# A decoder kernel turns its cross-attention contexts on VectorE and through DRAM instead of on TensorE

## The chip, the cores and the metric

The kernel runs on one core of a Trainium2 chip. The metric is the device time of one execution in microseconds; the time shown is the median of three runs. The profile is that of one further execution. Engines are named as in the profile: PE is TensorE (PEld its weight loads), DVE is VectorE, ACT is ScalarE, POOL is GpSimd, and SP is the engine whose queue issues all DMAs of this kernel.

## The reference

The reference is two decoder layers over `x` of shape (32, 56, 128), all in fp32. Both layers attend to the same context `ctx_1024` of shape (32, 1500, 128), and a layer normalization follows every block.

```
x = LN(x + windowed_self_attention(x))            # 16 heads of 8, window 32
x = LN(x + cross_attention_0(ctx, ctx, x))        # one head of 128, softmax over 1500 keys
x = LN(x + experts_0(x))                          # 8 experts of 512, top 2, gelu
x = LN(x + recurrent_mixer(x))                    # convolution, gates, a scan over 56 steps
x = LN(x + cross_attention_1(x, ctx))             # 16 heads of 64, softmax over 1500 keys
x = LN(x + experts_1(x))                          # shared expert and 8 of 256, top 2, silu
```

A context is the 1500 x 128 block of one of the 32 batches. Scores need it with the 128 features on the partitions ("turned"), and the weighted sum over keys needs it with the keys on the partitions, as it lies in DRAM.

## The kernel before

**Contexts.** A context is loaded as 125 partitions of 12 keys (`PK = 125`, `CK = 12`), key number 12p + c on partition p in chunk c, by `load_context` (two DMAs). `cxN` holds the two contexts of a pair for the first cross attention, `amN` those for the second one, each with a column of ones beside the 128 features, so that one product gives the weighted sum and the normalizer.

**Stages.** Two batches make a pair; there are 16 pairs. The groups are pair 0, pair 1, and then seven groups of two pairs (`GROUPS`). For each group a thread `pre` runs self attention, `cross_attention_0`, `experts_0`, the recurrent mixer and the queries of the second cross attention. The thread `attention` (called main) does the second cross attention for 32 batches in 64 blocks of 512 or 384 query columns: for each of 12 chunks a product of `amT` (the turned context, 125 columns of it as the stationary operand) and the queries gives scores `s`; maxima, exponentials and the products `v` with `amN` follow one block later. The thread `post` does the output projection and `experts_1`. The first two groups run in an opening of their own (`opening`), pair 1 in borrowed tiles ("aside", where `amN` takes the place of `cxN`).

**Order.** The threads are Python generators. A clock, `clock["pe"]`, adds up an assumed cost of each matmul; every `yield` of a thread gives a delay on this clock before which the thread is not resumed (`HOP`, `NORM`, `LOAD`), and `until` resumes `pre` as far as its share of `PRE_US` is due by the progress of main. Within what this writes down, the tile framework orders the instructions of each engine. [...]

**Turning.** `cross_attention_0` turns the two contexts of a pair with 12 transposes each (`tr`, L156 in the profile: the context is the stationary operand, an identity the moving one), four to a PSUM bank. Three copies per context, two on ACT and one on DVE (L518), bring them to `cxT`, which are the tiles `big0` and `big1`. A DMA stores each turned context to the DRAM tile `memT` (L520), from where `load_attended_T` fetches it into `amT` when the second cross attention comes to that batch (L1062). `amT` has one buffer. The score products of `cross_attention_0` (qpad, 500 columns each) read `cxT`; its probabilities `pr` overwrite `cxT[0]` and are turned back by 12 transposes into `pt`, which lies in `cxT[1]`. Then the 24 products with `cxN` follow, and the contexts of the next pair are loaded into `cxN`. The code of the score loop of main (`mm` is L147 in the profile):

```
ps = bank(p_s, "s")
mm(ps[:PK, :n], amT[:, c * PK : (c + 1) * PK], qT)
nc.scalar.copy(s[:, c, :], ps[:PK, :n])
```

Of the kernel before, what the change touches and what calls it, by code (L numbers as in the profile page):

```python
# [9 lines left out]
F32 = mybir.dt.float32  # L10
# [4 lines left out]
B, S, D, SK = 32, 56, 128, 1500  # L15
# [6 lines left out]
GROUPS = [[0], [1]] + [[p, p + 1] for p in range(2, NPAIR, 2)]  # L22
# [6 lines left out]
PK, CK = 125, 12  # L29
PSPLIT = 112  # L30
NS, CS = 3, 4
# [29 lines left out]
CYCLE = 1 / 2400  # L61
MATMUL_MIN, TRANSPOSE = 0.23, 0.145

PRE_US, POST_US, PAIR_US = 74.0, 31.0, 80.5
PROJECT_US = 3.6
BLOCKS = ((0, 512), (512, 384))

# [2 lines left out]
def decoder_kernel(  # L70
# [19 lines left out]
    nc = tc.nc  # L90
# [15 lines left out]
    def bank(pool, tag):  # L106
        if pool is p_f and place["aside"]:
            pool, tag = p_s, "s"
        return pool.tile([P, 512], F32, tag=tag, name=tag)
# [44 lines left out]
    def tr(ps, in_):  # L154
        k = in_.shape[0]
        nc.tensor.transpose(ps, in_, ident[:k, :k])  # L156
        clock["pe"] += TRANSPOSE
# [19 lines left out]
    n1 = const.tile([P, H1, D], F32, name="n1")  # L177


    cxN = [const.tile([PK, CK, D + 1], F32, name=f"cxN{i}") for i in range(2)]  # L180
    amN = [const.tile([PK, CK, D + 1], F32, name=f"amN{i}") for i in range(2)]
    amT = const.tile([P, CK * PK], F32, name="amT")
    for t in (*cxN, *amN):
        nc.gpsimd.memset(t[:, :, D : D + 1], 1.0)

    memT = [dram.tile([P, CK * PK], F32, tag=f"memT{b}", name=f"memT{b}") for b in range(B)]

    qo = [const.tile([P, 2, NQ], F32, name=f"qo{i}") for i in range(3)]

# [125 lines left out]
    def big_tile(i):  # L315
        return mid.tile([P, H0 * TP], F32, tag=f"big{i}", name=f"big{i}")
# [66 lines left out]

    HOP, NORM, LOAD = 2.5, 6.0, 14.0


    def self_attention(xs):
# [99 lines left out]
    def load_x0(pp):  # L489
        cxN = contexts_0()  # L490
        for i in range(2):
            b = 2 * pp + i
            load_context(cxN[i], b)

    def cross_attention_0(xs, g):
        nj, nt, nb = len(xs), len(xs) * TP, 2 * len(xs)
        cxN, qpad = contexts_0(), here(qpad0, "qpad")[:, :nb]
        xT = to_features(xs, "xT")
        res = [ahead(t, rowb("xbo0")) for t in xs]
        yield HOP  # L500
        qp, oT, vT = wide_tile("qT0", nt), wide_tile("oT0", nt), wide_tile("kT0", nt)
        affine(qp, linear(sqw("xq0"), xT, nt), vcol("xbq0"))
        yield HOP
        nc.scalar.mul(
            qpad[:, :, :S],
            linear(sqw("xk0"), qp, nt).rearrange("p (b s) -> p b s", b=nb),
            1.0 / math.sqrt(D),
        )
        w = CS * PK
        for p in range(nj):  # L510
            cxT = [big_tile(i) for i in range(2)]
            for i in range(2):
                for k in range(NS):
                    ps = bank(p_f, "f")
                    for c in range(CS):
                        tr(ps[:, c * PK : (c + 1) * PK], cxN[i][:, k * CS + c, :D])
                    copy = nc.vector.tensor_copy if k == 1 else nc.scalar.copy
                    copy(cxT[i][:, k * w : (k + 1) * w], ps[:, :w])  # L518
                    yield 0
                nc.sync.dma_start(memT[2 * GROUPS[g][p] + i], cxT[i][:, : CK * PK])  # L520
            yield 0.4


            pr = cxT[0]
            mx = tiny.tile([P, NS], F32, tag="mx", name="mx")
            for k in range(NS):
                ps = bank(p_f, "f")
                for i in range(2):
                    mm(
                        ps[64 * i : 64 * i + 64, :w], qpad[:, 2 * p + i, :],  # L530
                        cxT[i][:, k * w : (k + 1) * w],
                    )
                nc.scalar.copy(pr[:, k * w : (k + 1) * w], ps[:, :w])
                nc.vector.tensor_reduce(
                    mx[:, k : k + 1], pr[:, k * w : (k + 1) * w], AX.X, ALU.max
                )
                yield 0
            nm = tiny.tile([P, 1], F32, tag="nm", name="nm")
            nc.vector.tensor_reduce(nm, mx, AX.X, ALU.max, negate=True)
            for k in range(NS):  # L540
                nc.scalar.activation(
                    pr[:, k * w : (k + 1) * w], pr[:, k * w : (k + 1) * w], AF.Exp, bias=nm
                )
            yield 5.0
            pt = cxT[1][:PK, : CK * P].rearrange("p (c q) -> p c q", c=CK)
            for k in range(NS):
                ps = bank(p_f, "f")
                for c in range(CS):
                    lo = (k * CS + c) * PK
                    tr(ps[:PK, c * P : (c + 1) * P], pr[:, lo : lo + PK])  # L550
                copy = nc.scalar.copy if k == 1 else nc.vector.tensor_copy
                copy(
                    pt[:, k * CS : (k + 1) * CS, :],
                    ps[:PK].rearrange("p (c q) -> p c q", c=CS),
                )
                yield 0
            yield 0.8
            po = bank(p_f, "f")
            for c in range(CK):
                for i in range(2):  # L560
                    mm(
                        po[64 * i : 64 * i + 64, : D + 1], pt[:, c, 64 * i : 64 * i + 64],
                        cxN[i][:, c, :], start=(c == 0), stop=(c == CK - 1),
                    )
            rz = tiny.tile([P, 1], F32, tag="rz", name="rz")
            nc.vector.reciprocal(rz, po[:, D : D + 1])
            o = work.tile([P, D], F32, tag="ao0", name="ao0")
            nc.scalar.activation(o, po[:, :D], AF.Copy, scale=rz)
            if p + 1 < nj:
                load_x0(GROUPS[g][p + 1])  # L570
            elif 1 < g < NG - 1:
                load_x0(GROUPS[g + 1][0])
            yield 2.5
            ps = bank(p_f, "f")
            tr(ps[:, :P], o)
            nc.vector.tensor_copy(
                pair(oT, p).rearrange("p (b s) -> p b s", b=2),
                ps[:, :P].rearrange("p (b s) -> p b s", b=2)[:, :, :S],
            )
            yield LOAD if p + 1 < nj else HOP  # L580
        affine(vT, linear(sqw("xv0"), oT, nt), vcol("xbv0"))
        yield HOP
        ys = []
        for j in range(nj):
            ys.append(normalize(plus(linear(pair(vT, j), sqw("xo0"), D, TP), res[j]), "y"))
            yield 0
        yield NORM
        return ys
# [399 lines left out]
    def attention():  # L988
# [4 lines left out]
        for i in range(len(blocks) + 2):  # L993
            cur = None
            if i < len(blocks):
                b, q0, n = blocks[i]
                if q0 == 0:
                    if b % 2 == 0 and any(b // 2 == pairs[0] for pairs in GROUPS):
                        yield ("need", b // 2)
                s = sbig.tile([P, CK, n], F32, tag=f"s{n}", name=f"s{n}")[:PK]  # L1000
                m = mid.tile([P, 2, 512], F32, tag="m", name="m")[:PK, :, :n]
                qT = qo[(b // 2) % 3][:, b % 2, q0 : q0 + n]
                cur = (b, q0, n, s)
                for c in range(CK):
                    ps = bank(p_s, "s")
                    mm(ps[:PK, :n], amT[:, c * PK : (c + 1) * PK], qT)
                    nc.scalar.copy(s[:, c, :], ps[:PK, :n])  # L1007
                    if c % 2 == 1 and c > 1:
                        a = s[:, 0:2, :] if c == 3 else m
                        nc.vector.tensor_tensor(m, a, s[:, c - 1 : c + 1, :], ALU.max)  # L1010
                    if c % 2 == 0 and tail:
                        tail.pop(0)()
                    if c == 9 and old is not None:
                        outputs(old)
                        old = None
                    if c % 2:
                        yield 0
                nc.vector.tensor_tensor(m[:, 0, :], m[:, 0, :], m[:, 1, :], ALU.max)
                if q0 and b + 1 < B:
                    load_attended_T(b + 1)  # L1020
            elif old is not None:
                outputs(old)
                old = None
# [75 lines left out]
    def values(blk, t):  # L1099
        b, _, _, s = blk  # L1100
        po = bank(p_v, "v")
        for c in range(CK):
            mm(
                po[:, : D + 1], s[:, c, t * P : (t + 1) * P], amN[b % 2][:, c, :],
                start=(c == 0), stop=(c == CK - 1),
            )
            if c % 4 == 3:
                yield
        rz = tiny.tile([P, 1], F32, tag="rz1", name="rz1")
        nc.vector.reciprocal(rz, po[:, D : D + 1])  # L1110
        o = work.tile([P, D], F32, tag="ao", name="ao", bufs=5)
        nc.scalar.activation(o, po[:, :D], AF.Copy, scale=rz)  # L1112
        yield o
# [199 lines left out]
```

## Time and profile before

| | |
|---|---|
| time, median of three runs | 2333.89 us (2329.95 to 2337.73) |
| profiled execution: time | 2330.03 us |
| profiled execution: span of the core | 2328.3 us |
| mean granted TensorE clock | 0.984 |
| busy PE / PEld / DVE / ACT / POOL | 2214.2 / 1736.3 / 1437.5 / 1310.2 / 251.8 us |
| moved by DMA | 172.21 MB, 26.0% of 16 engines' span |
| transposes of `cxN` on PE (L156) | 360, busy 49.7 us |
| stores `memT<-big` | 30 of 750 KB |
| loads `amT<-memT` | 32 of 750 KB |

The page shows busy time by engine, then the span in 40 slices with the busy share of each in tenths, then groups of instructions: line, engine and operation, output and inputs with partitions x elements, count, busy time and mean duration of one, idle time of the engine ahead of them and what ended it. For a matmul the operands are written moving first and stationary second; an fp32 product is two PE instructions with two weight loads, a transpose is one. The durations of matmuls are latencies that overlap; busy time over count says what one of them takes in a stream.

### The profile page before, as it was taken

The page shows a single profiled execution, that of the slowest core. Times are in us where ns is not written, and L with a number is a line of the kernel's source. Part 1 is how long each engine was busy: PE and PEld are TensorE (multiplying, and loading weights), DVE is VectorE, ACT ScalarE, POOL GpSimd, SP SyncE. Part 2 cuts the span into 40 slices and gives each one's busy share as a digit, 9 for nine tenths or more (in the row PEclk, how much of TensorE's full clock was granted, in tenths as well). Part 3 has the DMA queues.
Part 4 walks back from the last instruction along what each step waited for, and adds up shares of the span by engine and source line. Part 5 has one row for each costly group of instructions (what it writes and reads, how often), then busy time and mean ns, then how long its engine had stood idle before and what let it go on. Part 6 is the DMA issues. An engine that isn't in the chain of part 4 may idle for free. (4 is left out here: it accounts for less than half of the span.)

```text
span 2328.3 us, 37425 instructions
## 1 busy us (share of the span) xinstructions
PE 2214.2 (95%) x14784; PEld 1736.3 (75%) x14784; DVE 1437.5 (62%) x2798; ACT 1310.2 (56%) x2279; POOL 251.8 (11%) x416
## 2 busy tenths in 40 slices
PE   7899998899999999999999999999999999999997
PEld 4766777577876788777887788768797778778787
DVE  4367554576366764676666665766656765566774
ACT  3455565556754667555655556564665555654652
POOL 3011001300023000210011100110001200100000
PEclk9899999999999999999999999999999999999999
DMA  6621322033311333114320153203331132211221
GB/s 185 178 74 29 107 54 86 16 81 91 97 48 30 80 104 105 29 36 126 92 76 17 54 134 91 65 14 81 107 111 32 28 107 71 68 27 41 69 83 37
DMA packets 164304, 172.21 MB, mean 74 GB/s; under 512 B 9465, under 2 KB 136865, under 8 KB 164001
## 3 DMA queue, kind: packets, MB, share of 16 engines
q1 hardware_dynamic: 164128, 169.82, 26.0%
q8 instruction: 117, 1.92, 0.3%
q14 instruction: 59, 0.48, 0.1%
HBM read 144.29 MB, written 25.49 MB: 73 GB/s over the span
## 5 line engine op out<-in xcount | busy, mean ns | idle before, releaser
L147 PE MATMUL v<-amN,s 125*128 125x129 f32 x5376 | 704.0, 277 | 6.1 <-ACT s L1095 3.6
L147 PEld LDWEIGHTS v<-amN,s 125*128 125x128 f32 x5376 | 665.4, 193 | 47.0 <-issue 25.6
L147 PE MATMUL s<-qo,amT 128*125 128x512 f32 (+1 forms) x1536 | 655.5, 547 | 3.4 <-ACT s L1007 3.1
L1007 ACT COPY s<-s 125x512 f32<-125x512 f32 (+1 forms) x768 | 396.8, 536 | 211.6 <-PE s L147 208.1
L1092 DVE TENSOR_TENSOR s<-s,nb 125x1536 f32<-125x1536 f32 (+1 forms) x256 | 395.4, 1556 | 61.8 <-ACT nb L1084 61.3
L1095 ACT ACTIVATE s<-s 125x1536 f32<-125x1536 f32 (+1 forms) x256 | 338.5, 1326 | 99.9 <-DVE s L1092 94.2
L147 PEld LDWEIGHTS s<-qo,amT 128*125 128x125 f32 x1536 | 264.7, 189 | 169.7 <-issue 94.5
L1010 DVE TENSOR_TENSOR m<-m,s 125x1024 f32<-125x1024 f32 (+1 forms) x256 | 280.8, 1097 | 79.4 <-ACT s L1007 75.5
L353 POOL TENSOR_SCALAR rs<-mv 112x1 f32<-112x1 f32 x126 | 44.2, 351 | 1562.9 <-DVE mv L347 1439.8
L1112 ACT ACTIVATE ao<-v,rz 128x128 f32<-128x128 f32 x224 | 80.5, 362 | 173.6 <-DVE rz L1110 170.4
L684 ACT ACTIVATE hT<-f,vec 128x224 f32<-128x224 f32 (+1 forms) x256 | 105.3, 435 | 100.9 <-PE f L147 98.4
L147 PE MATMUL f<-xT,wu 128*128 128x224 f32 (+1 forms) x512 | 135.6, 369 | 5.0 <-ACT hT L684 4.3
L147 PE MATMUL f<-wd,hT 128*112 128x128 f32 x960 | 126.2, 281 | 1.9 <-ACT hT L684 1.1
L147 PEld LDWEIGHTS f<-wd,hT 128*112 128x112 f32 x960 | 115.5, 181 | 15.4 <-ACT hT L684 3.9
L147 PE MATMUL f<-pxT,w 128*128 128x224 f32 (+1 forms) x576 | 119.4, 345 | 2.9 <-DMA w<-in_up_dram 1.1
L147 PEld LDWEIGHTS f<-pxT,w 128*128 128x128 f32 x576 | 98.7, 194 | 20.9 <-issue 4.4
L147 PEld LDWEIGHTS f<-xT,wu 128*128 128x128 f32 x512 | 86.7, 199 | 32.4 <-ACT hT L684 12.7
L1010 DVE TENSOR_TENSOR m<-s 125x1024 f32<-125x1024 f32 x64 | 69.6, 1087 | 54.3 <-ACT s L1007 54.2
L701 DVE SCALAR_TENSOR_TENSOR acc<-f,wmix,acc 112x128 f32<-112x128 f32 x120 | 41.6, 348 | 86.4 <-PE f L147 86.0
L444 POOL TENSOR_TENSOR big<-big,mx 112x448 f32<-112x448 f32 x60 | 75.5, 1276 | 146.4 <-PE f L147 71.0
L1084 ACT COPY nb<-t 125x512 f32<-125x512 f32 x64 | 34.0, 531 | 94.2 <-PE t L156 93.7
L156 PE MATMUL f<-ident,big 112*112 112x112 f32 (+1 forms) x420 | 62.8, 282 | 22.2 <-ACT big L448 15.6
(282 smaller groups left out, 2619.6 us busy)
## 6 DMA issues: line engine op xcount, KB each, us to landing
amT<-memT SPq DMA_DIRECT2D x32, 750.0 KB
amN<-in_mem_dram SPq DMA_DIRECT2D x34, 672.0 KB
memT<-big SPq DMA_DIRECT2D x30, 750.0 KB
cxN<-in_mem_dram SPq DMA_DIRECT2D x30, 672.0 KB
wu<-in_wup_dram SPq DMA_DIRECT2D x72, 256.0 KB
wd<-in_wdn_dram SPq DMA_DIRECT2D x72, 256.0 KB
w<-in_gate_dram SPq DMA_DIRECT2D x72, 128.0 KB
w<-in_up_dram SPq DMA_DIRECT2D x72, 128.0 KB
```

Source lines behind the costliest of these rows:

```text
L147: nc.tensor.matmul(ps, lhsT=lhsT, rhs=rhs, start=start, stop=stop)
L156: nc.tensor.transpose(ps, in_, ident[:k, :k])
L353: nc.gpsimd.tensor_scalar(rs, mv[:, 1:2], mul, add, ALU.mult, ALU.add)
L444: nc.gpsimd.tensor_tensor(s3[:, c, :], s3[:, c, :], mx[:, c].unsqueeze(2).to_broadcast([TP, 4, TP]), ALU.subtract,)
L684: nc.scalar.activation(hT[:, u, :], linear(ws[0][:, u * D : (u + 1) * D], xT, nt), AF.Gelu, bias=vec[:, C_BUP + e * nu + u : C_BUP + e * n ...
L701: nc.vector.scalar_tensor_tensor(acc[j], down(last[1], last[0][1], nu, j), w[:, j, e - 1 : e], acc[j], ALU.mult, ALU.add,)
L1007: nc.scalar.copy(s[:, c, :], ps[:PK, :n])
L1010: nc.vector.tensor_tensor(m, a, s[:, c - 1 : c + 1, :], ALU.max)
L1084: nc.scalar.copy(nb, ps[:PK, :n])
L1092: nc.vector.tensor_tensor(c, c, nb.unsqueeze(1).to_broadcast([PK, 3, n]), ALU.add)
L1095: nc.scalar.activation(c, c, AF.Exp)
L1112: nc.scalar.activation(o, po[:, :D], AF.Copy, scale=rz)
```

## The change

From the third pair on (groups of two pairs), a context is turned by two DVE instructions, which turn each square of 32 by 32 in place of its block; the squares then have to change places, which four stores to `memT` do (each takes 32 partitions and writes 1536-byte runs); one load brings the whole turned context back into the same tile. The order of the elements is now key by key with the 12 chunks inside, `[P, PK, CK]`, in `cxT`, `memT` and `amT`; so operands of one chunk step by 12 elements. The first two pairs keep the transposes, and their copies write in that order. `cxN` has 128 partitions, of which the last three are zero. `PRE_US` is 67 instead of 74, and the thread pauses for `TURN` = 10 on its clock after it has asked for the turns.

```diff
-PRE_US, POST_US, PAIR_US = 74.0, 31.0, 80.5
+PRE_US, POST_US, PAIR_US = 67.0, 31.0, 80.5
...
-    cxN = [const.tile([PK, CK, D + 1], F32, name=f"cxN{i}") for i in range(2)]
+    cxN = [const.tile([P, CK, D + 1], F32, name=f"cxN{i}") for i in range(2)]
-    amT = const.tile([P, CK * PK], F32, name="amT")
+    amT = const.tile([P, PK, CK], F32, name="amT")
+    for t in cxN:
+        nc.vector.memset(t[P - 32 :], 0.0)
...
-    memT = [dram.tile([P, CK * PK], F32, tag=f"memT{b}", name=f"memT{b}") for b in range(B)]
+    memT = [dram.tile([P, PK, CK], F32, tag=f"memT{b}", name=f"memT{b}") for b in range(B)]
...
-    HOP, NORM, LOAD = 2.5, 6.0, 14.0
+    HOP, NORM, LOAD, TURN = 2.5, 6.0, 14.0, 10.0
...
+    def turned(t, b, i):
+        big = big_tile(i)
+        u = big[:, : CK * P]
+        for r in range(2):
+            half = slice(r * CK // 2, (r + 1) * CK // 2)
+            nc.vector.transpose(
+                u.rearrange("p (f i c) -> p c f i", f=D // 32, c=CK)[:, half],
+                t[:, half, :D].rearrange("p c (f j) -> p c f j", j=32),
+            )
+        rows_of = memT[b].rearrange("(f j) k c -> j f (k c)", j=32)
+        for k in range(P // 32):
+            n = min(32, PK - 32 * k) * CK
+            nc.sync.dma_start(
+                rows_of[:, :, 32 * CK * k : 32 * CK * k + n],
+                u[32 * k : 32 * k + 32].rearrange("p (f n) -> p f n", f=D // 32)[:, :, :n],
+            )
+        u = u[:, : PK * CK]
+        nc.sync.dma_start(u, memT[b].rearrange("p k c -> p (k c)"))
+        return big
+
+    def turned_at_once(t, b, i):
+        big = big_tile(i)
+        u = big[:, : PK * CK]
+        u3 = u.rearrange("p (k c) -> p c k", c=CK)
+        for k in range(NS):
+            ps = bank(p_f, "f")
+            for c in range(CS):
+                tr(ps[:, c * PK : (c + 1) * PK], t[:PK, k * CS + c, :D])
+            copy = nc.vector.tensor_copy if k == 1 else nc.scalar.copy
+            copy(
+                u3[:, k * CS : (k + 1) * CS, :],
+                ps[:, : CS * PK].rearrange("p (c k) -> p c k", c=CS),
+            )
+            yield 0
+        nc.sync.dma_start(memT[b].rearrange("p k c -> p (k c)"), u)
+        return big
...
-            cxT = [big_tile(i) for i in range(2)]
+            cxT = []
             for i in range(2):
-                for k in range(NS):
-                    ps = bank(p_f, "f")
-                    for c in range(CS):
-                        tr(ps[:, c * PK : (c + 1) * PK], cxN[i][:, k * CS + c, :D])
-                    copy = nc.vector.tensor_copy if k == 1 else nc.scalar.copy
-                    copy(cxT[i][:, k * w : (k + 1) * w], ps[:, :w])
-                    yield 0
-                nc.sync.dma_start(memT[2 * GROUPS[g][p] + i], cxT[i][:, : CK * PK])
-            yield 0.4
+                b = 2 * GROUPS[g][p] + i
+                if g > 1:
+                    cxT.append(turned(cxN[i], b, i))
+                else:
+                    cxT.append((yield from turned_at_once(cxN[i], b, i)))
+            yield TURN if g > 1 else 0.4
...
-                    lo = (k * CS + c) * PK
-                    tr(ps[:PK, c * P : (c + 1) * P], pr[:, lo : lo + PK])
+                    tr(ps[:PK, c * P : (c + 1) * P], pr[:, k * CS + c :: CK])
...
-                    mm(ps[:PK, :n], amT[:, c * PK : (c + 1) * PK], qT)
+                    mm(ps[:PK, :n], amT[:, :, c], qT)
```

More of the change, by code (lines that the diff above doesn't have):

```diff
@@ L508, in cross_attention_0 @@
         )
-        w = CS * PK
         for p in range(nj):
-            cxT = [big_tile(i) for i in range(2)]
+            cxT = []
             for i in range(2):
-                for k in range(NS):
-                    ps = bank(p_f, "f")
-                    for c in range(CS):
-                        tr(ps[:, c * PK : (c + 1) * PK], cxN[i][:, k * CS + c, :D])
-                    copy = nc.vector.tensor_copy if k == 1 else nc.scalar.copy
-                    copy(cxT[i][:, k * w : (k + 1) * w], ps[:, :w])
-                    yield 0
-                nc.sync.dma_start(memT[2 * GROUPS[g][p] + i], cxT[i][:, : CK * PK])
-            yield 0.4
-            pr = cxT[0]
+                b = 2 * GROUPS[g][p] + i
[4 more added lines that the diff above has]
+            yield TURN if g > 1 else 0.4
+            pr = cxT[0][:, : PK * CK]
+            w = CS * PK
             mx = tiny.tile([P, NS], F32, tag="mx", name="mx")
@@ L562, in cross_attention_0 @@
                         po[64 * i : 64 * i + 64, : D + 1], pt[:, c, 64 * i : 64 * i + 64],
-                        cxN[i][:, c, :], start=(c == 0), stop=(c == CK - 1),
+                        cxN[i][:PK, c, :], start=(c == 0), stop=(c == CK - 1),
                     )
@@ L1103, in values @@
             mm(
-                po[:, : D + 1], s[:, c, t * P : (t + 1) * P], amN[b % 2][:, c, :],
+                po[:, : D + 1], s[:, c, t * P : (t + 1) * P], amN[b % 2][:PK, c, :],
                 start=(c == 0), stop=(c == CK - 1),
```

## The prediction

> **What bounds the kernel now.** I read first the page's busy shares and slices, then the groups by form, then what TensorE and SP's queue waited for, and last the order of events where contexts are turned.
>
> ```profile
> span 2328.3 us, 37425 instructions
> PE 2214.2 (95%) x14784; PEld 1736.3 (75%) x14784; DVE 1437.5 (62%) x2798; ACT 1310.2 (56%) x2279; POOL 251.8 (11%) x416
> PE   7899998899999999999999999999999999999997
> DMA  6621322033311333114320153203331132211221
> ...
> PE f L156 <- DVE h L356: 19.7, 17, 2.6
> PE f L156 <- ACT big L448: 15.6, 14, 4.7
> ```
>
> TensorE is busy 95% of the span and in nearly every slice. The longest of its waits comes to 19.7 us and all of them to about 100, and DMA engines are half idle or more from slice 4 on. So a microsecond taken from TensorE should be nearly a microsecond of the result, and work on other engines is free as long as its result is not late.
>
> ```profile
> L156 PE MATMUL f<-ident,cxN 125*128 125x125 f32 x360 | 49.7, 274 | 1.2 <-ACT qpad L504 0.7
> L156 PE MATMUL f<-ident,big 128*125 128x128 f32 x180 | 27.5, 285 | 0.2 <-ACT big L541 0.2
> L156 PEld LDWEIGHTS f<-ident,big 128*125 128x125 f32 x180 | 23.1, 187 | 9.5 <-DVE th L867 2.8 <-issue 2.1 <-ACT big L541 1.9
> L518 ACT COPY big<-f 128x500 f32<-128x500 f32 x60 | 34.4, 585 | 13.2 <-PE f L156 12.7
> L518 DVE COPY big<-f 128x500 f32<-128x500 f32 x30 | 20.3, 677 | 15.6 <-PE f L156 14.5 <-ACT big L518 1.0
> L147 PEld LDWEIGHTS v<-amN,s 125*128 125x128 f32 x5376 | 665.4, 193 | 47.0 <-issue 25.6 <-ACT s L1095 6.3 <-ACT ao L1112 3.1
> L147 PEld LDWEIGHTS s<-qo,amT 128*125 128x125 f32 x1536 | 264.7, 189 | 169.7 <-issue 94.5 <-ACT s L1007 26.4 <-ACT big L541 0.7
> L1010 DVE TENSOR_TENSOR m<-m,s 125x768 f32<-125x768 f32 x128 | 124.2, 970 | 40.7 <-ACT s L1007 38.0
> ```
>
> The first row is the work that goes: busy time over count is 49.7 / 360 = 0.138 us for one turn of a 125x128 square (the 274 ns is its latency; they overlap). The two LDWEIGHTS rows at the end are the weights whose layout changes or bears on it; a stream of them takes 665.4 / 5376 = 0.124 us each.
>
> ```profile
> 1201.13 3.60 PE L147 MATMUL s<-qo,amT 128*125 128x512 f32 x8
> 1201.56 0.19 PEld L147 LDWEIGHTS s<-qo,amT 128*125 128x125 f32 x1 [0.24 <-ACT s L1007]
> 1201.99 0.19 PEld L147 LDWEIGHTS s<-qo,amT 128*125 128x125 f32 x1 [0.24 <-issue]
> 1206.72 2.85 PE L147 MATMUL v<-amN,s 125*128 125x129 f32 x24
> 1206.72 2.65 PEld L147 LDWEIGHTS v<-amN,s 125*128 125x128 f32 x23 [0.24 <-issue]
> ...
> 1231.23 0.34 SPq L1062 DMA_DIRECT2D amT<-memT  x1
> ```
>
> In a run of scores a weight load of 0.19 us starts every 0.43 us and rests 0.24: it lies under the product before it. In the values stream (v) loads stand back to back, without rest. The amT load goes out at 1231.23; the timeline has the first product on it at 1249.99, so this load has some 15 us to spare.
>
> **The change, part by part.**
>
> *TensorE's turns (gain).* Seven groups of two pairs, two contexts each, twelve squares: 336 of the 360 go, 336 x 0.138 = 46.4 us. The stretch from 136 to 2270 us is 96.4% busy (2056.4 of 2134), so I take 45. Below, 35, if some of it only becomes waiting; above, 52, if waits for PSUM banks around these turns go too.
>
> *Copies that go.* Per context two ACT copies and one VectorE copy: ACT loses 56 x 0.585 = 33 us, VectorE 28 x 0.677 = 19. Neither bounds; counted as nothing.
>
> *VectorE's turns.* 56 instructions of 768 elements per partition. No row shows a turn. The nearest by size is L1010 with 768 elements, 0.97 us; the far end [...]: the row with 1536 elements (L1092) has 1.76. So VectorE gets 54 to 99 us, less the 19 removed: net 35 to 80, and goes to 63 or 65% busy. Behind each turn on VectorE stand maxima, additions and reciprocals of the attention. TensorE's waits on VectorE are about 50 us in all; 3 to 5% more load and single blocks of 1 to 1.8 us should add 2 to 15. I take 5.
>
> *The way through DRAM.* Per context 4 stores of 32 partitions and a load in place of one store: 112 stores and 28 loads against 28 stores, so SP issues 112 DMAs more at 0.33 to 0.43 us, and 21.5 MB more are moved. SP waits for VectorE's turn, then for the stores to land before the load; weights (wu, wd, w), amN, cxN and amT queue behind. For landing I use the timeline: the amT load of 1231.23 had its traffic between 1232 and 1235, so 3.5 us for 750 KB. Chain of one context: two turns 2 to 3.5, issue 1.3, store 3.5, issue and load 4, together 11 to 12; the second context some 4 later, 15 to 17. [...]
>
> Who waits: the score products on cxT. In the instruction order of the changed program, priced by the rows above, TensorE has 21 to 48 us of work between the last result that VectorE reads before a turn and the first product on it (the code asks for 10 us by its own clock, but VectorE's turns come ahead). So the chain is covered, narrowly in the shortest cases; without the cover it costs up to 14 pairs x 8 = 110. SP's queue is blocked for about 8 us per pair; before, it already stood up to 34.6 us on one memT store (SPq L520 <- DVE big L518), and amT has 15 us in hand. I take 3 us for late loads (bounds 0 and 30).
>
> *Layout.* amT and the turned context are now stored key by key, 12 chunks inside, so a stationary operand of 125 columns steps 12 elements, 48 bytes. That concerns all 1536 loads for the scores (768 products, two loads each) and 192 transposes of probabilities. No row before has such a load. Lower end: nothing, 0.124 us as now. Upper end [...] I estimate two, 0.248 us. Inside a run of scores that is still hidden (0.43 us per product, about 0.36 with 384 columns). It shows where a score product follows a short one: 245 of 768 in the changed order, each with 0.13 us of cover, 245 x 0.12 = 29 us; and in the transposes, 0.153 us each now (27.5 / 180), 192 x 0.10 = 19. Together 48. With the row the sum is unchanged[...]. I take the row: the fp32 loads run at 0.97 ns per column[...]. That is a choice, and it is the largest one here.
>
> *Small.* In the first two pairs the copies now write in steps; if ACT's double, 8 x 0.6 plus little: 2 us in the opening. Two memsets on VectorE precede the first cxN loads: about 1 us, partly hidden. I take 2 together. PRE_US (74 to 67) only keeps pace with the removed 7 us per group.
>
> *Sum* against the profiled execution (span 2328.3, time 2330.0): -45 + 5 + 3 + 2 = -35 with the weights free; I give back 3 for blocks of the order that fit worse, -32: 2298. The median of the runs shown is 3.9 above that execution, so 2302.
>
> **The rivals.**
>
> *Weight loads at half rate* (the case on the other side). Place: a score product behind a short one, and the transposes of pr. Price 48, so -32 + 48 = +16: 2350, between 2325 and 2370. It turns the result to slower from about 1.7 times the present 0.124 us on (437 x 0.085 = 37 less the slack). For it: [...] that 75% of the span has a load under way. Against it: 169.7 us of rest ahead of these loads. At three times or more, a load outlasts a 384-column product as well and the cost passes 130: 2430.
>
> *Turn late.* TensorE stands at the first score product of a pair. 5 to 10 us in 14 pairs give 70 to 140, less the gain: 2370 to 2440. For it: two DRAM trips and a queue that waits in order. Against it: 21 to 48 us of work in between.
>
> *VectorE as the limit.* If one turn costs 3 us, VectorE gets 150 net and each block is longer than most delays that the attention hides: about 1 us each, 56 in all: 2302 + 50 = 2352. Against: 0.97 us for 768 elements in any row.
>
> **How the numbers follow.** Weights free, turn covered: 0.47, 2284 to 2320. Half rate: 0.28, 2325 to 2370. Slower still, or a turn that is late: 0.17, above 2370. VectorE: 0.08, 2330 to 2370. This kernel's runs differ by 0.17% each way, so 0.3% (7 us, 2327 to 2341) is about what can be told from no change. Faster: 0.47 and 0.03 of half rate, 0.50; the same: 0.09; slower 0.41. The range leaves out part of the slowest case and a little below: 2284 to 2380; the likeliest case alone is 2284 to 2320.
>
> **What would show it.** cxN turns on TensorE x24, DVE turns x56 of 0.9 to 1.8 us, PE near 2168 us busy. LDWEIGHTS s<-qo,amT still about 189 ns, and pr's transposes 0.153 us each; if it is near 290 and PE is not below 2200, half rate it is. Waits of PE for DMA at qpad products: under 10 us; more, and the turn is late. Wrong altogether if PE is 46 us less busy and the span is not shorter.

## The result, and the profile after

The changed kernel takes 2436.9 us (median, 2434.2 to 2440.6) beside 2334.45 us of the kernel before on the same chip: ratio 1.0441, interval 1.0418 to 1.0465. The forecast was 2302 us with a range up to 2380. The change costs 102 us (103 by the ratio, which is used below) where I had expected it to save 32.

First the head of the page after: span, busy time of each engine with its share and number of instructions, and the span in 40 slices (tenths busy).

```profile
span 2436.7 us, 36970 instructions
PE 2290.1 (94%) x14448; PEld 1960.0 (80%) x14448; DVE 1499.5 (62%) x2828; ACT 1285.5 (53%) x2219; POOL 245.1 (10%) x416
PE   7899997999999999999999999899999999999998
DMA  6521432034312433035321244213421232211221
```

TensorE has 336 instructions fewer and is 76 us *more* busy (2214.2 before); its weight loads (PEld) are up by 224 us. That can't be a turn that comes late; it is the same work at a higher price. The groups by form name it (busy us and mean ns of one; then the idle time before them and what ended it):

```profile
L147 PEld LDWEIGHTS s<-qo,amT 128*125 128x125 f32 x1536 | 483.5, 345 | 66.5 <-ACT s L1047 14.2 <-issue 11.3 <-ACT big L574 4.0
L156 PEld LDWEIGHTS f<-ident,big 128*125 128x125 f32 x180 | 50.5, 359 | 4.6 <-ACT big L582 1.6 <-ACT big L592 0.9 <-issue 0.8
L147 PEld LDWEIGHTS v<-amN,s 125*128 125x128 f32 x5376 | 670.0, 195 | 56.8 <-issue 22.5 <-ACT s L1135 18.5 <-ACT ao L1152 7.8
L147 PE MATMUL s<-qo,amT 128*125 128x512 f32 x768 | 385.8, 625 | 1.1 <-ACT s L1047 1.0
L506 DVE STREAM_TRANSPOSE big<-cxN 128x768 f32<-128x768 f32 x56 | 83.7, 1531 | 8.3 <-PE f L156 4.5 <-ACT s L1047 2.4 <-DMA cxN<-in_mem_dram 1.3
L147 PE MATMUL f<-big,qpad 128*64 128x500 f32 x180 | 61.2, 599 | 0.3 <-DVE big L531 0.3
```

The first two rows are the loads that now step 48 bytes from column to column: 345 and 359 ns, where the same rows before read 189 and 187. The third, contiguous as ever, stands at 195 beside 193. The rest ahead of the score loads fell from 169.7 to 66.5 us. VectorE's turn, never seen before, takes 1531 ns. The last row's work is the same as before, yet it is busy 61.2 us; that is taken up below.

Then the waits: TensorE's (engine, what it waited for, us in all, times, longest), and two of SP's queue.

```profile
PE f L156 <- DVE h L359: 28.5, 22, 2.7
PE v L147 <- ACT s L1135: 15.7, 10, 3.3
PE f L156 <- DMA wu<-in_wup_dram: 2.4, 1, 2.4
...
SPq L513 <- DVE big L506: 125.3, 22, 14.8
SPq L518 <- DMA memT<-big: 67.0, 35, 6.3
```

The queue does stand behind the turns and the stores, as foretold, but no single wait of TensorE for a DMA that came with the change is longer than 2.4 us. All rows of TensorE's waits for DMA add up to 12.8 us (9.6 before), and none is at the products on the turned contexts. What grew are waits for VectorE (54.2 to 69.0) and ACT (40.3 to 56.1).

### The profile page after: what moved, and what is told of

Read it like the earlier page. It is cut to its first block, busy times and chain, and to the rows that moved or that the text cites. A ratio compares the mean times of both kernels' runs of the same rounds, so it can differ in the third digit from the quotient of the medians.

```text
span 2436.7 us, 36970 instructions
## 1 busy us (share of the span) xinstructions
PE 2290.1 (94%) x14448; PEld 1960.0 (80%) x14448; DVE 1499.5 (62%) x2828; ACT 1285.5 (53%) x2219; POOL 245.1 (10%) x416
## 4 chain that ended last, share of the span: by engine, by line
PE 69%; DVE 11%; ACT 6%; issue 6%; POOL 6%; DMA 2%; SPq 0%; POOLq 0%; DVEq 0%; ACTq 0%
PE f L147 25%; PE s L147 20%; PE v L147 18%; PE f L156 3%; PE t L156 3%; DVE s L1132 2%; DVE m L1050 2%; POOL rs L357 2%; ACT s L1135 2%; DVE big L506 2%; POOL big L447 2%; POOL rs L356 1%; ACT L724 1%; ACT L1135 1%; DVE big L439 1%
## 5 line engine op out<-in xcount | busy, mean ns | idle before, releaser
L147 PE MATMUL s<-qo,amT 128*125 128x512 f32 (+1 forms) x1536 | 700.4, 578 | 1.8 <-ACT s L1047 1.5
L147 PEld LDWEIGHTS s<-qo,amT 128*125 128x125 f32 x1536 | 483.5, 345 | 66.5 <-ACT s L1047 14.2
L1050 DVE TENSOR_TENSOR m<-m,s 125x1024 f32<-125x1024 f32 (+1 forms) x256 | 279.4, 1092 | 92.2 <-ACT s L1047 89.9
L356 POOL TENSOR_SCALAR rs<-mv 112x1 f32<-112x1 f32 x126 | 38.3, 304 | 1687.2 <-DVE mv L350 1537.9
L156 PEld LDWEIGHTS f<-ident,big 112*112 112x112 f32 (+1 forms) x420 | 76.7, 235 | 33.8 <-ACT big L451 17.8
L156 PE MATMUL f<-ident,big 112*112 112x112 f32 (+1 forms) x420 | 87.1, 340 | 17.4 <-ACT big L451 10.9
L1050 DVE TENSOR_TENSOR m<-s 125x1024 f32<-125x1024 f32 x64 | 69.7, 1089 | 49.4 <-ACT s L1047 49.2
```

The lines of the kernel that those rows point to most:

```text
L147: nc.tensor.matmul(ps, lhsT=lhsT, rhs=rhs, start=start, stop=stop)
L356: nc.gpsimd.tensor_scalar(rs, mv[:, 1:2], mul, add, ALU.mult, ALU.add)
```

## The experiments

Differences below are the ratio's excess times 2334 us, so that runs from different chips compare. "start to start" is the time from one TensorE instruction's start to the next one's in the trace, added up by kind; unlike busy time, it doesn't count overlaps twice.

**e1: the new order of elements alone.** TensorE's turns stay for all pairs, their copies write the stepped layout; no turn on VectorE, no trip through DRAM.

```diff
-PRE_US, POST_US, PAIR_US = 67.0, 31.0, 80.5
+PRE_US, POST_US, PAIR_US = 74.0, 31.0, 80.5
-                if g > 1:
+                if g > 99:
                     cxT.append(turned(cxN[i], b, i))
...
-            yield TURN if g > 1 else 0.4
+            yield 0.4
```

> The new element order alone: all contexts are turned by TensorE as before, and only the copies write key by key, so that amT and pr are read in steps of 12 elements. Theory L (the stepped weight loads are the loss): slower than before by at least the 77 us that the start-to-start times of score products (505 to 560 us) and transposes of pr (31 to 53 us) grew in the changed kernel; since that one also saved 46 us of turns and lost 102 in all, up to 150: 2410 to 2485 us. Theory T (the turn on VectorE and its two trips through DRAM are the loss): 2327 to 2345 us, since nothing of the turn is there.

Ratio 1.0353 (1.0338 to 1.0368): +82 us from the layout by itself, where theory L had put it. One cost in it is not the full change's: here the copies of all contexts write in steps (1061 ns on ACT in place of 585), there only those of the first two pairs.

```profile
L147 PEld LDWEIGHTS s<-qo,amT 128*125 128x125 f32 x1536 | 482.5, 345 | 63.5 <-ACT s L1047 13.8 <-issue 12.6 <-ACT nb L1124 0.7
L156 PEld LDWEIGHTS f<-ident,big 128*125 128x125 f32 x180 | 50.3, 360 | 5.8 <-DVE th L907 1.6 <-ACT big L582 1.0 <-issue 0.8
```

These are the two rows of after, without any of the rest of the change. Start to start, score products rise by 49 us and the transposes of the probabilities by 25, 74 of the 82; the turns of the contexts, behind their slower copies, by another 5.5. Where the 49 sit is plain in the trace: a score product that follows another one starts the next in 0.429 us (512 columns) as before; one that follows something *else* takes 0.579 in place of 0.429, and with 384 columns 0.474 in place of 0.327. Here a load of 345 ns hides under a score product and not under a short one.

**e4: a ruler.** Ahead of the kernel's work, streams of 16 weight loads with the elements of a column 1, 2, 3, 4, 6, 8 and 12 apart, and a few instructions of VectorE, into tiles that are overwritten later.

```diff
+    for _ in range(16):
+        nc.tensor.transpose(rp[:125, :128], ruler[:, : 125 * 2 : 2], ident)
...
+    for _ in range(6):
+        nc.vector.transpose(rq[:, :768].rearrange("p (c f i) -> p c f i", c=6, f=4), ruler[:, :768].rearrange("p (c f j) -> p c f j", c=6, f=4))
```

> The kernel before with a measuring stretch at its start that nothing uses: streams of 16 transposes and of 8 fp32 products whose stationary operand (128 x 125) steps 1, 2, 3, 4, 6, 8 and 12 elements; 8 products each whose moving operand steps 1, 4 and 12; VectorE turns of 768 elements with contiguous and with stepped writes; copies of 500 elements out of PSUM on VectorE and ACT with contiguous and with stepped writes. [...] If the distance matters, it grows from step to step. VectorE's turn: 0.97 us contiguous against 1.53 stepped if the writes are what makes it long; the same for both if the turn itself is.

The timeline of its weight loads (start, duration of the stretch, then the line; L303 steps 1, L305 2, L307 3, L309 4, L311 6, L313 8, L315 12):

```profile
19.82 1.82 PEld L303 LDWEIGHTS t<-ident,amT 128*125 128x125 f32 x16
21.57 1.93 PEld L305 LDWEIGHTS t<-ident,amT 128*125 128x125 f32 x16
23.41 2.80 PEld L307 LDWEIGHTS t<-ident,amT 128*125 128x125 f32 x16
26.13 3.75 PEld L309 LDWEIGHTS t<-ident,amT 128*125 128x125 f32 x16
29.78 3.57 PEld L311 LDWEIGHTS t<-ident,amT 128*125 128x125 f32 x16
33.26 3.83 PEld L313 LDWEIGHTS t<-ident,amT 128*125 128x125 f32 x16
36.99 4.31 PEld L315 LDWEIGHTS t<-ident,amT 128*125 128x125 f32 x16
41.20 0.98 PEld L317 LDWEIGHTS t<-ident,amT 128*125 128x125 f32 x8
```

From the starts, one load with the product behind it takes 0.109 us at step 1 and 0.115 at step 2 (1.84 / 16), 0.170 at step 3, 0.228 at step 4, 0.22 and 0.23 at steps 6 and 8, and 0.263 at step 12 (from 36.99 to 41.20). The time grows with the step, but not evenly: by 0.006 us to step 2, by 0.055 to step 3 and 0.058 to step 4, hardly further to step 8, and by another 0.03 to step 12. Against step 1, the step of 4 costs a factor of 2.1 and the step of 12 one of 2.4. Why, no run shows.

(The run's whole time, 2391.5 us, contains the ruler and is compared with nothing.) The same run priced VectorE's turn (contiguous writes, then stepped ones):

```profile
L338 DVE STREAM_TRANSPOSE n<-amT 128x768 f32<-128x768 f32 x6 | 5.9, 978 | 3.6 <-POOL amT L297 3.5
L340 DVE STREAM_TRANSPOSE n<-amT 128x768 f32<-128x768 f32 x6 | 9.3, 1545 | 0.2
```

**e2 and e3: the change without its stepped loads.** e2 reads `amT` in contiguous runs of 125 (the keys then go by chunk, so `amN` is loaded in that order, in runs of 512 bytes). e3 also lets the exponential read in steps and write its result chunk by chunk, so that the transposes of the probabilities read contiguous columns.

```diff
-                    mm(ps[:PK, :n], amT[:, :, c], qT)
+                    mm(ps[:PK, :n], amT.rearrange("p k c -> p (k c)")[:, c * PK : (c + 1) * PK], qT)
-        load_context(amN[b % 2], b)
+        rows_of = mem[b].rearrange("(c p) d -> p c d", p=PK)
...
+            ex = cxT[1][:, : PK * CK].rearrange("q (c p) -> q c p", c=CK)
-                    tr(ps[:PK, c * P : (c + 1) * P], pr[:, k * CS + c :: CK])
+                    tr(ps[:PK, c * P : (c + 1) * P], ex[:, k * CS + c, :])
```

> The changed kernel, with amT read in contiguous runs of 125: as the turned context lies in DRAM in the order of the keys, a run is the keys 125c to 125c + 124, and amN is loaded so that partition p holds key 125c + p in chunk c, in place of 12p + c. The turn on VectorE stays, and so do the stepped transposes of pr. Theory L: 1536 of 1728 stepped loads go, LDWEIGHTS of scores back to about 189 ns, and 85 to 110 us come back: 2325 to 2350 us. Theory T: 2430 to 2445 us, as the changed kernel.

> As the one with contiguous reads of amT, and the transposes of pr read contiguously too: the exponentials of the first cross attention are written chunk by chunk into the other tile of the pair (ACT reads in steps instead). No stepped weight load is left except none. Theory L: another 20 to 30 us, 2295 to 2325 us, which is the predicted gain of the turn without its layout. Theory T: 2430 to 2445 us.

e2: ratio 1.0346 (1.0330 to 1.0361), +81 us. e3: 1.0282 (1.0265 to 1.0299), +66 us. Both lie between the two theories' numbers and fit neither.

```profile
L147 PEld LDWEIGHTS s<-qo,amT 128*125 128x125 f32 x1536 | 265.8, 188 | 177.9 <-issue 94.3 <-ACT s L1050 27.8 <-ACT big L574 4.2
L156 PEld LDWEIGHTS f<-ident,big 128*125 128x125 f32 x180 | 23.4, 187 | 19.2 <-ACT big L583 8.0 <-DVE th L910 3.7 <-DVE big L595 2.8
L583 ACT ACTIVATE big<-big,nm 128x500 f32<-128x500 f32 x45 | 50.1, 1177 | 1.1 <-DVE nm L581 1.0
```

These are three rows of e3. The loads are back at 188 and 187 ns, so the stepped loads are out of it. The third row is what e3 pays for that: the exponential now reads in steps and takes 1177 ns, where the same row of the kernel before has 703, so ACT has 21 us more to do. This stays in all runs below that build on e3, and no run took it out. The scores' part of the layout is 22 us here (after less e2), the transposes' 15 (e2 less e3, with the slower exponential against it), and e3 is still 66 us slower than before with the turns gone from TensorE. My theory that the layout was the whole of it fell here. A second cause of about 100 us, counted from the forecast, was open, and the remaining runs look for it.

**x1, x2: e3 with the turn taken out.** The tiles, and `amT` too, are loaded straight from the contexts from the third pair on, untransposed. x1 keeps the pause of 10 us, x2 sets it to 0.4. What else e3 changed (the order in which `amN` is loaded, the place of the exponential) stays in both.

```diff
+    def flat_of(b):
+        return mem[b].rearrange("k d -> (k d)").rearrange("(p a) -> p a", p=P)
...
-        nc.sync.dma_start(u, memT[b].rearrange("p k c -> p (k c)"))
+        nc.sync.dma_start(u, flat_of(b))
...
-            yield TURN if g > 1 else 0.4
+            yield 0.4
```

> The kernel of e3 (no stepped weight loads, 2397 us) with the turn left out: the tiles that the score products read are loaded straight from the contexts in DRAM, whatever lies there, so the contexts are not transposed from the third pair on. Gone are the 56 VectorE turns (1.53 us each) and the four stores per context; the pause of 10 us and the order on TensorE stay. Before is about 2332, and 46 us of turns are gone in both. Theory V (VectorE's turns, or SP's queue behind them, cost the 65 us that e3 is above before, and swallowed the 46): about 2290. Theory P (the pause that waits for the turn is the cost: it empties one stretch and crowds the next): 2380 to 2397, little gained.

> As x1, and the pause between the loads and the first score product is 0.4 us of the planner's clock in place of 10. The tiles are still loaded, so TensorE may now wait for those loads (two of 768 KB, some 4 us, 14 pairs: up to 56 us). Theory P: below x1 by 40 to 100 us, less what those waits cost. Theory V: no faster than x1.

x1: ratio 0.9983 (0.9975 to 0.9991), -4 us. x2: 0.9933 (0.9916 to 0.9950), -16 us. Theory V is the nearer one, but x1 is 39 us above its 2290, and x2's gain is far from theory P's 40 to 100. So what makes the turned contexts is worth 70 us (e3 less x1), and the pause 12. And x2 is about the most that the idea could bring in this schedule: with the turns gone and nothing in their place but loads it gains 16 us (it still carries e3's slower exponential). TensorE's turns took 41.0 us start to start before and take 4.5 here; of the 36.5 us that are gone, TensorE's waits (all rows) give back 15 (104.8 to 119.9: ACT +10, VectorE +5), and the opening some 4 (the first score product at 140.4 us against 135.9; the stepped copies of the first two pairs stand there). The pause is seen as waits as well: from x1 to x2 they fall by 14 us, 12 of them for VectorE.

**x3, x4: the pause and VectorE's turns alone, on the kernel before.**

```diff
-            yield 0.4
+            yield 10.0 if g > 1 else 0.4
```

```diff
+                if g > 1:
+                    for r in range(NS):
+                        part = slice(r * CS, (r + 1) * CS)
+                        nc.vector.transpose(
+                            scr.rearrange("p (f i c) -> p c f i", f=D // 32, c=CS),
+                            cxN[i][:, part, :D].rearrange("p c (f j) -> p c f j", j=32),
+                        )
```

> The kernel before, with TensorE's turns and its layout, and one number changed: from the third pair on the pause after the turns is 10 us of the planner's clock in place of 0.4. All outputs are as before. Theory P: slower than before by 40 to 110 us (2370 to 2440). Theory V: within 10 us of before (2332).

> The kernel before, with VectorE's turns added and nothing taken away: after TensorE's turns, each context is also turned by VectorE, three instructions of 512 elements with stepped writes, into a tile that nobody reads (84 instructions, about 86 us of VectorE in all; the order on the other engines stays). Theory V: slower by 40 to 110 us. Theory P: 0 to 15 us.

x3: ratio 1.0040 (1.0025 to 1.0055), +9 us. x4: 1.0136 (1.0121 to 1.0152), +32 us.

```profile
L527 DVE STREAM_TRANSPOSE scr<-cxN 128x512 f32<-128x512 f32 x84 | 93.6, 1114 | 11.2 <-DMA cxN<-in_mem_dram 10.4
```

The theory of the pause is out as the main cause. That of VectorE holds in part: with its result read by nobody, and VectorE still at 64% of the span, 94 us of turns make the kernel 32 us longer, about 0.34 us for each us of turns. TensorE's waits for VectorE go from 54.2 to 71.8 us. x4 falls just short of what I had set down for that theory (40 to 110).

**y1, y2, y3, y4: the 70 us taken apart.** y1: e3 with the turn writing contiguously (the elements land elsewhere). y2: x1 with the turns put back, the load waiting for them, no stores. y3: e3 without turns, the stores taking the context as loaded. y4: e3 with the stores of both contexts ahead of both loads. The diff shows y1's edit, then y3's.

```diff
-                u.rearrange("p (f i c) -> p c f i", f=D // 32, c=CK)[:, half],
+                u.rearrange("p (c f i) -> p c f i", f=D // 32, c=CK)[:, half],
...
-                u[32 * k : 32 * k + 32].rearrange("p (f n) -> p f n", f=D // 32)[:, :, :n],
+                t[32 * k : 32 * k + 32].rearrange("p c d -> p (c d)")[:, : CK * P].rearrange(
+                    "p (f n) -> p f n", f=D // 32)[:, :, :n],
```

> The kernel of e3 (2397 us), but VectorE's turn writes its squares chunk after chunk, in contiguous runs, so the elements land in another order (the squares are turned, their places are not the ones that the later steps expect). In the ruler a turn of 768 elements took 0.98 us in this way and 1.55 with stepped writes: 56 turns, 31 us less on VectorE; stores, loads, pause and order stay. Leaving out turns, stores and the trip through DRAM gave 68 us (x1). If VectorE's time is the price, a third of its share comes back: 10 to 25 us below e3. If the way through DRAM is the price: within 6 us of e3.

> x1 (2329 us; tiles loaded straight from the contexts, untransposed, pause kept) with VectorE's turns put back: the turn writes the tile, and the load that overwrites it waits for the turn, but there are no stores and no wait for them to land. If VectorE's turns are the price of the 68 us between x1 and e3: 2380 to 2397. If the stores are: 2329 to 2345. x4 (turns alone on the kernel before, +31 us) would make it about 2360.

> e3 with VectorE's turns left out and all else kept: the four stores per context take the rows of the context as they were loaded, the load waits for the stores, pause and order stay (the contexts are not transposed). If the stores and the queue behind them are the price: 2380 to 2397. If the turns are: 2329 to 2345. If both share it as x4 has it: about 2365.

> e3 with one change of order in SP's queue: the stores of both contexts of a pair go out ahead of both loads, so that the second context's stores no longer wait for the first one's load. In e3 the two 64-column halves of a score product on the turned contexts run one after the other in the second pairs (58.9 us in all against 43.5 in x1), which would mean that the second load is late. If lateness of the second context is part of the price: 10 to 25 us below e3 and that row back near 44 us. If not: within 6 us of e3.

| run | turns on VectorE | stores, load waits for them | ratio | against before |
|---|---|---|---|---|
| x1 | none | none | 0.9983 (0.9975 to 0.9991) | -4 us |
| y2 | yes | none | 1.0086 (1.0064 to 1.0108) | +20 |
| y3 | none | yes | 1.0134 (1.0107 to 1.0161) | +31 |
| y1 | contiguous writes | yes | 1.0165 (1.0146 to 1.0184) | +39 |
| y4 | yes | yes, other order in the queue | 1.0255 (1.0240 to 1.0271) | +60 |
| e3 | yes | yes | 1.0282 (1.0265 to 1.0299) | +66 |

Turns alone cost 24 us over x1, stores alone 35, both 70. Both share it, with 11 us more together than apart (plus or minus 9, from the four intervals). y1 is the cleanest of these: in its trace the instructions of every engine stand in exactly e3's order; only the turn is shorter.

```profile
L506 DVE STREAM_TRANSPOSE big<-cxN 128x768 f32<-128x768 f32 x56 | 52.9, 961 | 8.5 <-PE f L156 4.5 <-ACT big L462 2.3 <-DMA cxN<-in_mem_dram 1.7
```

31 us less of turns (83.8 in e3) make the kernel about 27 us faster, a little more than I had set down; TensorE's waits fall by 18 (164.2 to 145.8), 15 of them for VectorE. y4 is a miss: six us at the edge of the two intervals, and its products on the turned contexts are not repaired (58.5 us busy against 61.4). y2 and y3 came out near the 2360 and 2365 us that a shared cause would make.

**z1: stores that nobody waits for.** y3's stores stay, the load takes its data straight from the source. (Only the load of `amT`, much later, still reads what they wrote.)

```diff
-        nc.sync.dma_start(u, memT[b].rearrange("p k c -> p (k c)"))
+        nc.sync.dma_start(u, flat_of(b))
```

> y3 (2365 us: stores, no turns) with one dependency cut: the four stores per context still go out, through the same queue and with the same bytes, but the load that follows takes the context straight from its source and waits for none of them (the contexts are not transposed). The order of TensorE's instructions, which the planner moved for 14% of them between x1 and y3, is then x1's again but for 4%. If the stores' traffic and their places in the queue are the price of the 35 us between x1 and y3: 2355 to 2370. If the dependency is, through the later landing and the order that the planner makes of it: 2329 to 2342.

Ratio 1.0030 (1.0021 to 1.0039), +7 us: 11 above x1 and 24 below y3. The traffic and the places in the queue are at most 11 of the 35 us; the dependency is the other 24. It isn't a wait for DMA (13.0 us in y3, 11.0 in x1). It comes with the order: the tile framework orders TensorE's instructions by its own estimate of when each result is there, and between x1 and y3 it moved 14% of them (6793 of 7883 keep a common order; between x1 and y2 it is 7854, between x1 and z1 7548). One trace of that is a row of x1, of y3 and of z1:

```profile
L147 PE MATMUL f<-big,qpad 128*64 128x500 f32 x180 | 44.8, 599 | 0.4 <-DVE big L521 0.3
```

```profile
L147 PE MATMUL f<-big,qpad 128*64 128x500 f32 x180 | 58.7, 600 | 0.3 <-DVE big L526 0.3
```

```profile
L147 PE MATMUL f<-big,qpad 128*64 128x500 f32 x180 | 45.0, 599 | 0.3 <-DVE big L529 0.3
```

The products of a pair's two contexts fill 64 columns of TensorE each. Side by side, they start 0.01 us apart and share 0.42 to 0.47 us (before). In y3, e3 and after, the second context is thought to come later; its products are put some 10 us behind in the second pair of a group, and each half pays 0.42 to 0.47 us (after) for itself: 13 us. What makes up the other 11 us of the dependency, in which stretches carry more of the layer's small products at a time and TensorE waits longer for ACT (61.8 us against 51.0), was not isolated. (y3's trace is of its slowest run, 10 us above its median.)

**The clock, a cost inside these terms.** One thing grew that no run was made for. The traces record stretches in which TensorE is granted half of its clock: 76 us in all before, 113 in after, 108 in e3, 97 in x1, 74 in x2, 70 in e1. The products `v`, which the change leaves alone, follow each other in 0.112 us at the full clock and in 0.214 at half of it. From after, two rows of the timeline, then the busy time of `v` in the stretch of the second one (0.50 is the granted clock):

```profile
1185.89 1.61 PE L147 MATMUL v<-amN,s 125*128 125x129 f32 x12 [1.25 <-ACT s L1135]
1190.78 2.52 PE L147 MATMUL v<-amN,s 125*128 125x129 f32 x10 [3.29 <-ACT s L1135]
...
1188.60:1195.40 6.80, 3.15 (x12) 2.77 (x12) 0.00 (x0) 0.00 (x0) 0.50 0.00 0
```

Most such stretches come behind waits. After has 18 of them between 136 and 2270 us, the kernel before 9; in the 3.4 us ahead of 16 of the 18, TensorE had stood still for about 1.5 us or more, where an average 3.4 us of this part holds 0.17 us of waiting. If such waits bring the half clock on, which no run isolated, they cost a second time. TensorE's work at half clock rose from 63 us before to 97 in after; by estimate half of the difference, up to 17 us, is lost by it (12 in e3, 7 in x1, none in x2 and e1). This is no further term, it lies within the differences above. No run here changed the clock alone, so its share is an estimate.

## Why the prediction was wrong, point by point

The forecast missed by 135 us (from -32 to +103), and two steps of it failed. One is the layout term, put at nothing: 82 us alone, 37 in the full change. The other is the premise that a microsecond off TensorE is nearly a microsecond gained while work on other engines is free: the turn without its layout was to save 32 us and costs 66 (e3), which is the other 98.

*The layout failed as the choice it was.* I had the row (0.124 us) and an estimate of twice that (0.248), and took the row. The ruler has 0.109 against 0.263. The row was contiguous and so said nothing of a step. Neither the factor of two nor putting the term at nothing had a measurement behind it. The mechanism of the rival was right to the place: the loss sits where a score product follows something short. Its size was not: 387 such places in the trace of after where I counted 245, and 0.12 us each as I had it, so 48 us in place of 29; the transposes 24 in place of 19. Together 72 to 74, not 48. The prediction's own sign for this case (loads near 290 ns, PE not below 2200 us) read 345 ns and 2290 us. Alone this costs 82 us (e1). On top of the turn's losses it adds 37 (after less e3): longer loads then seem to fill time in which TensorE waited anyway, 164.2 us in e3 and 138.6 in after, and e3 has the slower exponential to carry.

*TensorE's turns (45 us).* They went, as written (24 left). But 36.5 us start to start was the size to take, not the busy time of 46.4, and the time fell by 16 (x2). "A microsecond taken from TensorE should be nearly a microsecond of the result" did not hold here: with TensorE 95% busy, 15 of the 36.5 us came back as waits for ACT and VectorE in x2, a part of them perhaps through the slower exponential. The bound "below, 35" was too high.

*VectorE's turns (5 us).* The duration was in the bounds (0.97 to 1.76; it is 1.53), the price of it was not (2 to 15). 24 us when added to x1, 32 on the kernel before, 27 for a third of it in y1. Between 0.3 and 0.9 us per us of VectorE; why this price varies so is open. What grows is TensorE's waits for VectorE (in x4 from 54.2 to 71.8 us). The likely reason, not isolated, is that turns of 1.5 us stand in one queue with the maxima and additions that TensorE's next work needs. The rival "VectorE as the limit" named the mechanism, but asked for 3 us per turn; half was enough.

*The way through DRAM (3 us).* The turn was not late: no wait of TensorE for it, so the cover of 21 to 48 us held. Four stores of 32 partitions moved 197 to 259 GB/s (after, 501 to 504 us), the load behind them up to 420; a store of 128 partitions moved 378 to 426 in the kernel before (1089 to 1092 us). Yet stores and dependency cost 35 us (y3). The bound of 30 was passed, and the working missed how: I looked for a wait, and 13 us of the price were paid in order, in the split halves. Some 11 us are the stores themselves (z1), the last 11 are open.

*Pause, small terms.* The pause had no term; it costs 12 us in x2 to x1 and 9 alone. The opening was to take 2 us more; the first score product comes 7 us later in after (142.9 us against 135.9), 4 in x2. How much of that is the stepped copies was not isolated.

*The sum as measured*, each against the step before it: turns gone -16, pause +12, VectorE +24, stores +35, both together +11, stepped transposes +15, stepped scores +22: +103. The trace of after gives the same loss another way. Start to start and without waits, TensorE's time changes by +48 us for scores, +25 for the transposes of the probabilities, +15 for the split halves and -37 for the turns; its waits add 34. That is 85 of the 108 us between the two profiled executions, and the rest is spread over work that the change does not touch; by the estimate above, up to 17 us of the whole are the halved clock.

No version here beats the kernel before except x1 and x2, which don't turn the contexts from the third pair on.

## What to carry to other kernels

Ask of each operand that a layout change touches what step its innermost read has; where fp32 columns of a weight load lie 16 to 48 bytes apart, as in the ruler, count the loads that no long product hides and price each at about double (0.228 us at 16 bytes, 0.263 at 48, against 0.109). Where one engine is 95% busy and waits for others in a chain, don't count all that leaves it as gain, and don't count work on the others as free: here 16 of 36.5 us were gained, and VectorE, at 62%, cost 0.3 to 0.9 us for each us that was added to it. And compare the *order* of the instructions before and after as well as the waits: a dependency that is hardly waited for can still cost (24 us between z1 and y3), through the place at which the planner puts the work behind it.

## What the runs showed of the hardware

In the ruler, a weight load of 125 fp32 columns with a product of 128 columns behind it took 0.109 us at a step of 4 bytes, 0.115 at 8, 0.170 at 12, 0.228 at 16 and 0.263 at 48. VectorE's turn of 768 fp32 elements in squares of 32 took 0.98 us with contiguous writes and 1.55 with writes 48 bytes apart; a copy of 500 elements from PSUM took 0.68 us with contiguous writes (before) and 1.05 with writes 48 bytes apart (e1) on VectorE, 0.59 and 1.06 on ACT. ACT's exponential of 500 elements took 0.70 us with contiguous reads and writes (before) and 1.18 with reads 48 bytes apart (e3). So the step of 48 bytes cost a factor of 1.5 to 1.8 in these instructions. Two products of 64 columns each, side by side, took 0.42 to 0.47 us together (before); apart, each took 0.42 to 0.47 (after). Stretches at half clock, in which a product `v` took 0.214 us in place of 0.112, came mostly where TensorE had just stood still for about 1.5 us or more of 3.4 us (after).
